# Keys and values of eight batches at a time in seven products, and every block's queries in seven products

## The chip, the core and the metric

The kernel runs on one core of one Trainium2 chip. The core has five engines that run side by side, each with its own queue of instructions worked off in order: TensorE (PE in the profile; its weight loads are listed as PEld), VectorE (DVE), ScalarE (ACT), GpSimd (POOL) and SyncE (SP), which here only issues DMA transfers. GpSimd issues a few transfers as well. The metric is the time of one execution on the device in microseconds (us), lower is better. An instruction waits, by semaphores, until what it reads is written and what it overwrites has been read.

## The reference

A cross-attention layer in float32 with 16 batches, 1024 query rows and 64 context rows per batch, width 512, 16 heads of 32:

```python
def _ada_ln(x, c, W_ss, b_ss):
    h = (x - mu) / jnp.sqrt(var + EPS)            # over the width
    ss = jax.nn.silu(c) @ W_ss + b_ss
    scale, bias = jnp.split(ss, 2, axis=-1)
    return (1.0 + scale)[:, None, :] * h + bias[:, None, :]

xq  = _ada_ln(x_q,  t_vec, Wss_q,  bss_q)         # 16 x 1024 x 512
xkv = _ada_ln(x_kv, t_vec, Wss_kv, bss_kv)        # 16 x   64 x 512
q = (xq @ Wq + bq).reshape(B, Lq, nh, dh)
kv = (xkv @ Wkv + bkv).reshape(B, Lkv, 2, nh, dh) # keys, then values
scores = jnp.einsum('bqhd,bkhd->bhqk', q, k) / jnp.sqrt(jnp.float32(dh))
attn = jax.nn.softmax(scores, axis=-1)
out = jnp.einsum('bhqk,bkhd->bqhd', attn, v).reshape(B, Lq, H)
return x_q + (out @ Wp + bp)
```

## The kernel before

**Tiling.** The 16x1024 query rows are cut into 32 blocks of 512 rows, two per batch, numbered 0 to 31. Keys and values are made for two batches at a time (128 context rows). All products are float32; a TensorE instruction of the program shows as two passes in the profile, so that four instructions of 256 columns are "x8".

**A block's path.** `load_x` brings the rows in. `q_stats` takes mean and variance on VectorE (L263, L264), `q_scale` makes the reciprocal deviation (two ScalarE steps, then four small ones), `hidden` normalises on ScalarE (L324). `turn` transposes 32x32 squares on VectorE (L503) and `move` brings the squares to their partitions in 16 transfers (L516), so that the features lie on partitions. `scale_features` puts in the batch's scale and shift (L573). Then the queries (`query_product` and what stands with it, L633 to L670), `scores` (two halves, each followed by a maximum on VectorE, L703, and a copy out of PSUM on ScalarE, L712), `maxima` (L725, L734), `subtract` on GpSimd (L747), `weights` (the exponential, L753), `total` (L792), `row_total` and `inverse_rows` (L797, L812, and a way through DRAM, L815 and L817), `mix` (the second attention product, `po`, L861), `spread_rows` and `divided` (L823, L841), and the projection (`product` and `added`, L976 and L1000), which adds into the residual that `load_residual` brought, and writes out.

**Seven products.** Queries (from block 4) and projections (all but block 29's) are made by a 2x2 scheme of seven half-size products in the place of eight, with sums of quarters of the weights (`query_weight_sums`, `weight_sums`, once) and of the features (`feature_sums`, four GpSimd additions per block, L608 to L611). Two PSUM banks hold running results; `query_out` reads them out on ScalarE, `query_added` adds on VectorE. Blocks 0 to 3 use the plain form (`queries`, L546): sixteen instructions of 512 columns. Blocks 0 and 1 use weights that already hold the batch's scale (`query_weights`), with the shift's part in the bias (`query_bias_rows`, L464).

**Keys and values before.** Per pair of batches: a load, a statistic as fifth entry beside a block's four, `context_hidden`, four transposes (L351, `pkt`), a scaling on VectorE (L369) and a shift on GpSimd (L373), 16 instructions for the keys (L398, `pk`), 64 small ones for the values (L434, `pv`), and additions of the biases (L409, L447). In the loop a pair is spread over four blocks, one step in each (`kv` 0 to 3).

**Order.** Everything is written out by hand and each engine works its queue in the order written; no scheduler moves anything. Blocks 0 to 3 have an order of their own; from block 4 on a loop runs:

```python
for i in range(4, NB - 2):
    a, b, n, f = i - 1, i - 2, i + 1, i + 2
```

In turn `i` TensorE does scores of block `i`, queries of block `n`, the second attention product and the start of the projection of block `a`, and the rest of the projection of block `b`, while the other engines prepare blocks `f`, `i + 3` and `i + 4`. A tail handles blocks 30 and 31. PSUM has two pairs of banks (pool `ps_s`) that scores and the second attention product take in turn, and four single banks (`mm0` to `mm3`).

## Time and profile before

| | |
|---|---|
| median of 3 runs | 1040.41 us (1039.51 to 1040.89) |
| span of the profiled execution, from its first to its last instruction | 1038.5 us |
| what lies around the span, by the median | 1.9 us |
| PE busy | 1019.3 us, 98% |
| DVE busy | 854.9 us, 82% |
| POOL busy | 780.9 us, 75% |
| ACT busy | 610.6 us, 59% |
| granted TensorE clock | 1.00 |
| HBM | 79.02 MB read, 34.60 MB written |

The page gives the profiled execution its span alone; its own time is read as the span and the 1.9 us that the median of the runs stands above it. A line of groups reads: source line, engine, operation, tiles written and read, shapes, count, then busy time, the mean of one, and the idle time of the engine just before with what ended it. The chain that ended last is followed back from the last instruction of the run; each of its pieces has a start, a length, and what ran or was waited for. "issue" is time for which the profile shows no reason.

### The profile page before, as it was taken

Reading aid. Unit: us, or ns where it says so; the run is one execution under the profiler, and the core shown is the slowest. Engines: PE = TensorE matmul, PEld = TensorE weight load, DVE = VectorE, ACT = ScalarE, POOL = GpSimd, SP = SyncE. Lnnn points to the kernel's source line nnn. Section 1 sums busy time; section 2 is a strip of 40 time slices with the busy share of each in tenths; the row PEclk is TensorE's granted clock in tenths of the full one; section 3 lists DMA queues with packets and bytes.
Section 4 is the critical chain, followed back from the end, with each engine's and each line's share of the span. In section 5 each row is a group of like instructions: output and inputs, shape, how many; then the busy total and the mean of one; then the engine's idle time right before and its main releaser. Section 6 shows DMA issues by size and latency. Waiting matters only on the chain.

```text
span 1038.5 us, 22968 instructions
## 1 busy us (share of the span) xinstructions
PE 1019.3 (98%) x9058; PEld 759.5 (73%) x9058; DVE 854.9 (82%) x1159; ACT 610.6 (59%) x945; POOL 780.9 (75%) x502
## 2 busy tenths in 40 slices
PE   6999899999999999999999999999999999999998
PEld 4535577778777778778778787777787778777756
DVE  5889978987798887897979877998778987776794
ACT  3666756665566745675657666566566665565530
POOL 0579786886978867988668986688886886977861
PEclk9999999999999999999999999999999999999999
DMA  9841555343455333545334445344444453235122
GB/s 338 262 150 62 164 168 182 117 154 117 144 173 164 118 101 135 165 160 164 102 105 163 155 150 160 100 136 146 140 158 138 127 158 112 100 123 165 45 85 85
DMA packets 103500, 147.65 MB, mean 142 GB/s; under 512 B 33464, under 2 KB 34640, under 8 KB 103392
## 3 DMA queue, kind: packets, MB, share of 16 engines
q1 hardware_dynamic: 102368, 144.08, 43.4%
q0 software_dynamic: 1024, 2.10, 0.9%
q8 instruction: 72, 1.18, 0.5%
q14 instruction: 36, 0.29, 0.1%
HBM read 79.02 MB, written 34.60 MB: 109 GB/s over the span
## 4 chain that ended last, share of the span: by engine, by line
PE 84%; DVE 7%; DMA 3%; POOL 3%; ACT 1%; issue 1%; SPq 0%; DVEq 0%; POOLq 0%
PE pp L976 34%; PE pq L633 33%; PE po L861 6%; PE ps L684 6%; PE pv L434 2%; PE pk L398 2%; DMA x<-in_x_dram 2%; DVE m L703 1%; DVE bs L263 1%; DVE l L758 1%; DVE vb L823 1%; DVE lt L797 1%; DMA vr<-ltd 1%; DVE ot L841 1%; DVE r L1000 0%
## 5 line engine op out<-in xcount | busy, mean ns | idle before, releaser
L747 POOL TENSOR_TENSOR s<-s,mb 128x2048 f32<-128x2048 f32 x62 | 281.3, 4561 | 167.3 <-DVE mb L734 163.3
L712 ACT COPY s<-ps 128x1024 f32<-128x1024 f32 x128 | 129.3, 1012 | 106.3 <-DVE m L703 67.0
L703 DVE TRANSPOSE_TENSOR_REDUCE m<-ps 128x32 f32<-128x1024 f32 x128 | 150.9, 1215 | 29.8 <-PE ps L684 27.6
L976 PE MATMUL pp<-w_p_sb,ot 128*128 128x256 f32 x744 | 171.0, 380 | 1.1 <-DVE ot L841 0.7
L1000 DVE TENSOR_TENSOR r<-pp,r 128x512 f32<-128x512 f32 x210 | 136.2, 670 | 30.3 <-PE pp L976 24.1
L663 ACT ACTIVATE qt<-pq,bias_t 128x256 f32<-128x256 f32 x224 | 92.4, 463 | 116.1 <-PE pq L633 116.1
L976 PEld LDWEIGHTS pp<-w_p_sb,ot 128*128 128x128 f32 x744 | 141.3, 190 | 21.7 <-issue 1.7
L753 ACT ACTIVATE s<-s 128x2048 f32<-128x2048 f32 x64 | 122.3, 1911 | 46.4 <-POOL s L747 44.4
L792 POOL TENSOR_TENSOR sum<-s,s 128x2048 f32<-128x2048 f32 x30 | 136.2, 4541 | 5.5 <-ACT s L753 5.5
L976 PEld LDWEIGHTS pp<-WT,s 128*128 128x128 f32 x496 | 89.7, 190 | 57.0 <-issue 34.4
L976 PE MATMUL pp<-WT,s 128*128 128x256 f32 x496 | 123.1, 391 | 0.4 <-POOL s L955 0.2
L976 PE MATMUL pp<-WT,ot 128*128 128x256 f32 x496 | 117.7, 381 | 1.2 <-POOL ot L952 1.2
L633 PE MATMUL pq<-xt_sums,wq_sums 128*128 128x256 f32 x448 | 108.5, 386 | 0.0
L633 PE MATMUL pq<-xt,w_q_sb 128*128 128x256 f32 x448 | 106.3, 380 | 2.1 <-ACT pq L645 1.8
L633 PEld LDWEIGHTS pq<-xt_sums,wq_sums 128*128 128x128 f32 x448 | 83.0, 190 | 32.4 <-issue 22.4
L633 PE MATMUL pq<-xt,wq_sums 128*128 128x256 f32 x448 | 106.6, 381 | 0.0
L976 PEld LDWEIGHTS pp<-WT,ot 128*128 128x128 f32 x496 | 94.0, 190 | 16.9 <-POOL ot L952 2.5
L324 ACT ACTIVATE x<-x,rstdq 128x512 f32<-128x512 f32 x128 | 96.5, 807 | 3.1 <-DVE rstdq L294 1.9
L670 DVE TENSOR_TENSOR qt<-pq,qt 128x256 f32<-128x256 f32 x112 | 42.1, 418 | 66.2 <-PE pq L633 65.7
L633 PEld LDWEIGHTS pq<-xt,w_q_sb 128*128 128x128 f32 x448 | 85.0, 190 | 15.1 <-ACT pq L645 2.2
L263 DVE BATCH_NORM_STATS2 bs<-x 128x6 f32<-128x512 f32 x128 | 86.9, 679 | 9.5 <-DMA x<-in_x_dram 9.5
L633 PEld LDWEIGHTS pq<-xt,wq_sums 128*128 128x128 f32 x448 | 83.6, 190 | 11.8 <-issue 1.2
(128 smaller groups left out, 1581.1 us busy)
## 6 DMA issues: line engine op xcount, KB each, us to landing
x<-in_x_dram SPq DMA_DIRECT2D x32, 1024.0 KB, 5.8
r<-in_x_dram SPq DMA_DIRECT2D x32, 1024.0 KB, 5.6
out_dram<-r SPq DMA_DIRECT2D x60, 512.0 KB, 3.7
xt<-ht SPq DMA_DIRECT2D x464, 64.0 KB, 2.0
wss_q<-in_L_xcond_Wss_q_dram SPq DMA_DIRECT2D x2, 1024.0 KB, 8.0
ctx<-in_ctx_dram SPq DMA_DIRECT2D x8, 256.0 KB, 3.3
wss_kv<-in_L_xcond_Wss_kv_dram SPq DMA_DIRECT2D x2, 1024.0 KB
w_kv_sb<-in_L_xcond_Wkv_dram SPq DMA_DIRECT2D x1, 2048.0 KB
```

The costliest lines, as they stand in the source:

```text
L263: nc.vector.bn_stats(bs, r)
L324: nc.scalar.activation(dst, src, AF.Identity, bias=rstd[:, 1, j : j + 1], scale=rstd[:, 0, j : j + 1])
L633: nc.tensor.matmul(qa[k][:, m * HT : (m + 1) * HT].rearrange("p (g n) -> p g n", g=2), lhsT=a[:, c, m * P : (m + 1) * P], rhs=x[:, :, c, : ...
L663: nc.scalar.activation(dst, src, AF.Identity, bias=bq_t[:, o : o + 1])
L684: nc.tensor.matmul(pss[r // 2][32 * c : 32 * c + 32, r % 2, :], lhsT=kt[rows, c, z * HK : (z + 1) * HK], rhs=qt[rows, c, :], start=True, s ...
L703: nc.vector.tensor_reduce(m_tiles[i][:, z, 2 * e : 2 * e + 2, :], pss[e].rearrange("p r (j a) -> p r j a", a=32), AX.X, ALU.max, apply_tra ...
L712: nc.scalar.copy(s_sb[:, 2 * e : 2 * e + 2, :], pss[e])
L747: eng.tensor_tensor(s_tiles[i, z], s_tiles[i, z], mb_tiles[i], ALU.subtract)
L753: nc.scalar.activation(p, p, AF.Exp, scale=SCALE)
L792: nc.gpsimd.tensor_tensor(t, s_tiles[i, 0], s_tiles[i, 1], ALU.add)
L976: nc.tensor.matmul(acc[k][:, t * HO : (t + 1) * HO], lhsT=rows[:, c, t * P : (t + 1) * P], rhs=cols[:, c, :], start=n == 2 and t == 0 and ...
L1000: nc.vector.tensor_add(r, a, r)
```

## The change

Context rows are treated like query blocks. Group A is batches 0 to 7, group B batches 8 to 15; each has 512 context rows and is loaded by `load_x`, has statistics and is normalised as a block. Keys and values of a group are made with seven products each (`seven`, `context_steps`), 28 sets of four instructions in all, and kept on chip (`K_all`, `V_all`) to the end. Group A's features are transposed by TensorE and scaled by VectorE as they leave PSUM (`turned_features`, `turned_scaled`, `group_affine`); group B's go the way of a block (`turn`, `move` with every second transfer on GpSimd's queue, then eight VectorE operations, `group_affine`). The values come out of the products in another order of partitions; they are put into a staging tile and brought to their places in 16 transfers per group (`value_move`). The steps of group A stand ahead of and among the queries of block 0, those of group B behind them and in the loop's places that have no projection yet. All queries are made in seven products; block 0's features are transposed by TensorE (`turned_queries`). The loop starts at block 0; the pair steps in it are gone. Block 0's projection takes the plain form into banks that hold the bias (`project_seed`, `project_seeded`); `weight_sums` moves to turn 1. The order of the loads changes, and several tiles share room: the key weights, value weights and their sums lie in buffers that scores and residuals use later, and the staging tiles in that of the projection's weight sums.

```diff
-    load_x(0)
-    load_scale_shift("q", w_ss_q)
-    nc.sync.dma_start(w_q_sb, w_q.rearrange("(c p) o -> p c o", p=P))
-    load_context(0)
-    load_x(1)
-    load_scale_shift("kv", w_ss_kv)
-    nc.sync.dma_start(w_kv_sb, w_kv.rearrange("(c p) o -> p c o", p=P))
+    load_x("A")
+    load_scale_shift("kv", w_ss_kv, 0)
+    load_biases()
+    load_scale_shift("kv", w_ss_kv, 1)
+    load_context_weights(0)
+    load_value_bias()
+    load_context_weights(1)
+    load_x(0)
+    load_scale_shift("q", w_ss_q, 0)
+    load_scale_shift("q", w_ss_q, 1)
...
+    def turned_scaled(i, t, pt):
+        xk = xt_tiles[i].rearrange("p g c (t b) -> p g c t b", t=NT)
+        src = pt.rearrange("p (c j n) -> p c j n", c=NC, j=2)
+        b = GROUPS[i] * PER + 2 * t
+        for j in range(2):
+            scale = ss["kv"][:, :NC, b + j : b + j + 1].unsqueeze(3).to_broadcast([P, NC, 2, 32])
+            nc.vector.tensor_tensor(
+                xk[:, 2 * j : 2 * j + 2, :, t, :].rearrange("p z c b -> p c z b"),
+                src[:, :, j, :].rearrange("p c (z b) -> p c z b", z=2),
+                scale,
+                ALU.mult,
+            )
+
+    def group_affine(i, g, shift, eng):
+        xk = xt_tiles[i][:, g].rearrange("p c (t b) -> p c t b", t=NT)
+        s = group_batches(i, NC if shift else 0, g // 2)
+        s = s.unsqueeze(3).to_broadcast([P, NC, NT, 32])
+        eng.tensor_tensor(xk, xk, s, ALU.add if shift else ALU.mult)
...
+    def value_move(i, m):
+        for c in (2 * m, 2 * m + 1):
+            for t in range(NT):
+                nc.sync.dma_start(
+                    V_all[i][32 * c : 32 * c + 32, 2 * t : 2 * t + 2],
+                    stages[i][32 * t : 32 * t + 32, c].rearrange("p (j z) f -> p j z f", j=2),
+                )
+
+    def context_steps(i, name, banks):
+
+        ks, vs = (key_out, key_added), (value_out, value_added)
+        out_, add_ = ks if name == "k" else vs
+        for n in (1, 2, 6, 7, 5, 4, 3):
+
+            def step(n=n):
+                seven(i, name, n, banks)
+                if i == "A" and n == 1:
+                    out_(i, n)
+                elif i == "A" and n == 2:
+                    add_(i, n)
+                elif n == 1:
+                    seed(i, name, banks)
+                elif n in OUTS:
+                    out_(i, n)
+                else:
+                    add_(i, n)
+
+            yield step
...
+    feature_sums("A", nc.vector)
+    both_of()
+    both_of()
     q_stats(0)
     q_scale(0)
     hidden(0, range(NT))
+    next(KA)()
     scale_shift_rows("q", 0)
     scale_shift_rows("q", 1)
+    scale_shift_taken("q")
+    next(VA)()
+    scale_shift("q", 0)
+    q_stats("B")
+    both_of()
+    turned_queries()
+    column_sums("q", w_q_sb, w_q_sums, nc.gpsimd)
+    load_x(1)
+    q_scale("B")
+    feature_sums(0)
+    both_of()
+    hidden("B", range(NT))
+    turn("B", range(NT))
+    move("B", two=True)
     load_x(2)
+    both_of()
     q_stats(1)
+    both_of()
+    query_product(0, 1)
+    query_seed(0)
     q_scale(1)
     hidden(1, (0, 1))
+    for g in range(2):
+        group_affine("B", g, False, nc.vector)
+        group_affine("B", g, True, nc.vector)
+    query_product(0, 2)
+    query_out(0, 2)
     hidden(1, (2, 3))
     turn(1, range(NT))
+    move(1, two=True)
...
+    next(KB)()
+    scale_features(1, (0, 1))
+    next(KB)()
+    scale_features(1, (2, 3))
+    feature_sums(1)
+    next(KB)()
     hidden(2, range(NT))
...
-    for i in range(4, NB - 2):
+    for i in range(NB - 2):
...
+        def slot(j, m):
+            if j > 0:
+                product(j, m)
+            elif j == 0:
+                if m in (1, 2, 6, 5):
+                    project_seeded(0, (1, 2, 6, 5).index(m))
+            else:
+                step = next(KB, None) or next(VB, None)
+                if step is not None:
+                    step()
         scores(i, 0, crossed=True)
+        if i == 0:
+            turn(2, range(NT))
+            move(2)
+            load_x(4)
-        product(b, 6)
-        added(b, 6)
+        slot(b, 6)
+        add(b, 6)
...
-        if kv == 1:
-            context_scaled(kvb)
-        if kv == 2:
-            key_products(kvb, spare(f"pk_{kvb}"))
-        if kv == 3:
-            value_products(kvb, spare(f"pv_{kvb}"))
...
         query_product(n, 5)
         query_added(n, 5)
+        if i == 0:
+            turn(3, range(NT))
+            load_x(5)
         if i + 4 < NB:
             q_stats(i + 4, (2,))
...
         query_product(n, 4)
         query_added(n, 4)
```

## The prediction

> **What bounds the kernel now.** I read the page's engine shares first, then the chain that ended last, then its pieces in order of time, then the busy time of four stretches. Page and chain:
>
> ```profile
> span 1038.5 us, 22968 instructions
> PE 1019.3 (98%) x9058; PEld 759.5 (73%) x9058; DVE 854.9 (82%) x1159; ACT 610.6 (59%) x945; POOL 780.9 (75%) x502
> PE 84%; DVE 7%; DMA 3%; POOL 3%; ACT 1%; issue 1%; SPq 0%; DVEq 0%; POOLq 0%
> ```
>
> TensorE's busy share is modelled, so the pieces of the chain (start, us, what) have to confirm it. `po` is a block's second attention product, one per block; the first here is block 3's, the last block 28's:
>
> ```profile
> 168.67 2.28 PE po L861 x62
> 197.85 2.28 PE po L861 x62
> 200.13 1.93 PE pq L633 x8
> 205.51 1.73 PE pq L633 x8
> 227.48 2.28 PE po L861 x62
> 236.86 3.57 PE pk L398 x32
> 260.24 2.28 PE po L861 x62
> 269.62 3.63 PE pv L434 x128
> 293.25 2.28 PE po L861 x62
> 945.49 2.28 PE po L861 x62
> ```
>
> From one `po` to the next: 29.18 us for a block that makes no keys or values, 32.76 and 33.01 for those with `pk` and `pv`. The differences, 3.58 and 3.83, are the TensorE pieces themselves: nothing else sets a block's length. So in the loop TensorE's instructions are the time. The stretches (columns: length, then PE, PEld, DVE, ACT, POOL busy, clock, DMA, GB/s) show where that is not so:
>
> ```profile
> 0.00:16.70 16.70, 7.07 (x91) 5.76 (x91) 7.12 (x25) 6.02 (x11) 0.70 (x6) 1.00 0.85 307
> 16.70:154.50 137.80, 134.82 (x1196) 81.35 (x1195) 118.99 (x175) 85.28 (x138) 99.43 (x85) 1.00 0.56 178
> 154.50:932.50 778.00, 777.84 (x6985) 602.85 (x6984) 654.43 (x880) 481.99 (x753) 613.37 (x380) 1.00 0.44 139
> ```
>
> Until 16.7 the loads are all that moves; 154.5 is the first score product of block 4, where the regular loop begins. VectorE is at 86% in the second stretch: it is the engine with the least room while the pipeline fills.
>
> **The change, part by part.** Sums are against the profiled span, 1038.5; the median of the timed runs, 1040.41, is 1.9 above it, and I carry that 1.9 over.
>
> TensorE work. (1) Removed from the loop: six pairs of batches. Block 3's `po` to block 28's is 776.82 us; 25 blocks at 29.18 are 729.5, so the six cost 47.3 (7.9 each). Two more pairs, in the opening, at 0.43 (`pkt`) + 3.57 + 3.63: 15.3. (2) Added: 4 sets (two groups, keys and values) of seven products; a set is 6x1.73 + 1.93 = 12.3 (the loop's query set): 49.2; group A's 16 transposes at 0.43 per four: 1.7. (3) Queries of blocks 0 to 3: the plain form took 14.00 per block (piece at 47.85, 32 passes), seven products 12.3: -6.8. (4) The query-bias product of L464 goes (-1.1); block 0's projection becomes the plain form, 14.0 for 12.3 (+1.7). Net: -62.6 + 50.9 - 6.8 + 0.6 = -17.9. All of it is on the path, if TensorE is kept fed.
>
> The additions of keys and values are priced by L670 (418 ns) and L409 (658 ns). The other engines in the loop lose work (L369, L409, L447, L373 and a statistic): worth nothing, since the 29.18 blocks are TensorE's without them.
>
> The opening. Before, TensorE runs from 16.7 to 154.5 with 132.0 of work (4x14.0 + 12.3 queries, 15.3 keys and values, 8.6 scores, 6.8 `po`, 29.8 projections, 3.2 small): 5.8 us of waits. After, the work up to block 4's first scores is 132.0 - 6.8 + (49.2 - 15.3) + 0.6 + 1.7 (block 0's transposes, which ran before 16.7 and now run behind the first keys; group A's run before its first product) = 161.4. I lay the queues out with before's row times:
>
> - Start. Loads drain in order at about 3.0 us per MB: block 2's x had 10.25 MB issued up to its end and landed at 33.7.
>
> ```profile
> 16.82 16.92 DMA x<-in_x_dram
> ```
>
> The context's second scale-and-shift weight is the third MB: 12.2. Then 1 us of rows, 12 transposes, the bias add, eight 0.41 us scalings (price of L670's 418 ns) and two shifts put the first key product at 20.5. Cost: +3.8.
> - Block 0's scale rows wait for a VectorE copy. VectorE: POOL's two shifts done 22.6, four sums to 25.9, three additions to 28.2, block 0's statistics (4x0.77) to 31.3, its scale (two ScalarE and four VectorE steps, 1.5) 32.8, the copy 33.2; TensorE is there at 32.7: 0.5.
> - Block 1's x is issued when block 0's transposes free its buffer (38.8) and lands at 44.5; its statistics stand behind group A's additions (48.7 to 51.8), its scale ends at 53.2, and hidden(1), four steps of 0.81, stands on ScalarE between the query_out of block 0 (0.46 each). Block 0's products, 1.73 apart from 49.2, wait 0.6 for the seed, 0.8 for the first copy out, 0.8 for the second: 2.2.
> - Group B: its features move half by POOL's queue (8 DMAs, 3.91 us in before's row, 4.9 to landing), then eight VectorE affines, then POOL's feature sums (4x1.27) behind the eight DMAs of block 1's move. In numbers: turn(B) done 47.3, POOL's moves landed 56, affines to 57.7 and 64.1, turn(1) 60.5, its POOL DMAs to 64.5, third sum 68.3; the product is due at 67.4: 0.9.
> - scores(0, 1) needs the PSUM pairs of scores(0, 0), whose copies stand on ScalarE behind hidden(2): block 1's odd moves land at 69.4, its scaling and group B's outs run to 74.6, hidden(2) to 77.8, two copies (1.01) to 79.8; the scores are due at 76.3: 3.5.
> - Block 0's turn of the loop. VectorE carries two blocks' statistics (6.2), two turns (5.4), maxima (7.5), both groups' additions and a row total (2.8): about 28 us in a 31 us turn, in order. POOL's subtractions run from 86.4 (2x4.56), the second exponential ends at 97.4, the query_out behind it at 98.3: product 4 (due 96.5) is 1.8 late. Half a scaling and hidden(3) end at 103.1, turn(3) at 103.9, a statistic and query_added(1, 4) at 105.5: scores(1, 0), due 103.5, 2.1 late. A statistic, an addition, row_total(0) and its reciprocal (4.3) stand ahead of the maxima (2.5), which end at 112.4: scores(1, 1), due 110.1, 2.3 late. Together 6.2.
> - Block 1's turn: maxima, spread of the maxima and of the inverse sums (2.3 each) and two `ot` halves (1.22) end at 124.2; the seeded projection is due at 122.7: 1.5. Block 1's `ot` is 0.8 late in the same way.
> - Transfers. SP's sixteen issues of a move take 10.35 us in the loop; the two value moves add 32 issues of the same size (64 KB), 20.7 us of SP. Ahead of block 4's x and block 0's residual they make these land at about 95 and 130, 0 to 2 us after need, on VectorE and not on TensorE: 0.
>
> ```profile
> 314.63 10.35 SPq L516 DMA_DIRECT2D xt<-ht  x16
> ```
>
> Waits: 0.5 + 2.2 + 0.9 + 3.5 + 6.2 + 2.3 = 15.6. Block 4's scores then start at 20.5 + 161.4 + 15.6 = 197.5, 43.0 later than before. The rest loses 47.3, and block 4's own 1.2 over a regular block (30.4 between its scores and the next) may go too; I count half. Sum: +43.0 - 47.3 - 0.6 = -4.9: span 1033.6, time 1035.5.
>
> Unshown costs. VectorE's all-SBUF 128x512 operations (two shifts, four sums, eight affines): from 0.67 (L1000, one operand in PSUM) to 0.84 (a quarter of L747's 3342 ns); taken near the middle; ends -1 and +1 us on the path. The waits together: from before's 5.8, if the order hides as well as before's, to twice mine, 31: the end moves by -9.8 and +15.6. I take 15.6, since each of its terms follows from a row and an in-order queue, and keep the ends for the range. The start: from 18.5 (no queueing of the small loads) to 23: -2 and +2.5.
>
> What VectorE's all-SBUF work does to POOL is seen at one place: while VectorE ran its only two subtractions, POOL's fourth weight sum took 3.32 for a usual 1.27.
>
> ```profile
> 53.92 6.61 DVE L747 TENSOR_TENSOR s<-s,mb 128x2048 f32<-128x2048 f32 x2
> 55.06 3.32 POOL L918 TENSOR_TENSOR WT<-w_p_sb,WT 128x512 f32<-128x512 f32 x1
> 58.35 2.78 POOL L919 TENSOR_TENSOR b_diff<-b_p_sb 128x256 f32<-128x256 f32 x1
> ```
>
> With L919 (2.78; half of 1.27 by size) POOL lost some 4.2 us in 6.6. The change adds about 10 us of such VectorE work, so POOL may lose 6; group A's part hides (the value sums are due 4 us later), group B's 3 falls on its feature sums or block 1's DMAs: 0 to 3 us, taken as 0, since the affines mostly end before POOL's work starts. [...]
>
> **The rivals.**
>
> A. The order hides the fill (waits 5.8 as before): 1035.5 - 9.8 = 1026. For it: queues laid out by hand serialise more than the chip does. Against it: three of the waits come from in-order queues, whatever the durations.
>
> B. Slower, by POOL's queue. Group B's and block 1's odd moves go through it in a row: landing 4.9 is a median of 32, and SP's own moves reach 8.1. If POOL's take 8.1 too, group B's last affine and turn(1) slip 3.2, block 1's features another 3.2, hidden(2) and the copies of scores(0, 0) by 6.4, and TensorE with them; with the 3 us that VectorE may take from POOL, by 9.4: 1045. It decides from a slip of 7.0, which puts the time 2.1 past before's 1040.4; below that it only eats the gain. For it: nothing else in the opening can run meanwhile, as TensorE's order has only group B's products there. Against it: group B's features have 5 us of slack at their first product, and the landing is a median.
>
> C. The loop's blocks do not fall to 29.18, another engine being just behind. The 29.18 blocks are in this trace, with VectorE at 84%: 0.05 at most; at 29.5 the 25 blocks would add 8: 1043.
>
> **How the numbers follow.** A change of 0.2% (2.1 us) is about what a measurement of this kernel tells from none. Forecast (1029 to 1038): 0.46; A: 0.20; B: 0.25, a fifth of it within the bound; C: 0.05; a near miss of the forecast between 1038.3 and 1042.5: 0.04. Faster 0.66, same 0.09, slower 0.25. Range: below, A with the early start and the rest of block 4's 1.2, 1023; above, B with contention and 2 us, 1047.
>
> **What would show it.** Key and value groups of 28 products in all, none after block 1; `po` 29.2 apart from block 4 on, everywhere; first key product near 20.5; block 4's scores near 198. Before that, TensorE idle ahead of scores(0, 1) released by ScalarE's copies, ahead of scores(1, 0) by VectorE. Wrong if scores(4, 0) stands past 202 (slower) or before 190 (A), or if a regular block is not 29.2.

## The result, and the profile after

The changed kernel is 0.5% slower: median 1047.03 us of 12 runs, against 1040.97 of the kernel before, beside it on the same chip; the ratio is 1.0051, interval 1.0038 to 1.0064. The forecast was 1035.5.

The page of the changed kernel (span, engine shares, PE and granted clock in forty slices, the chain by engine):

```profile
span 1044.6 us, 21070 instructions
PE 1007.0 (96%) x8025; PEld 759.3 (73%) x8025; DVE 877.8 (84%) x1184; ACT 628.1 (60%) x980; POOL 806.4 (77%) x504
PE   3988899999999999999999999999999999999997
PEclk8999999999999999999999999999999999999999
PE 83%; DVE 5%; DMA 3%; SPq 3%; ACT 2%; POOL 2%; issue 1%; DVEq 0%; POOLq 0%
```

TensorE has 12.3 us less work than before (1019.3) in a span 6.1 us longer. The dents of PE's row, and the clock's only one, lie in the first five slices (26 us each). The pieces of the chain in order of time:

```profile
4.04 7.04 DMA early<-in_L_xcond_bss_kv_dram
18.34 5.38 issue
23.72 3.71 PE pk_A L504 x8
27.43 1.73 PE pv_A L504 x8
...
220.72 2.42 PE po L798 x63
...
951.19 2.28 PE po L798 x62
```

220.72 is block 3's second attention product, 951.19 block 28's: 730.5 us, where the kernel before took 776.82. The loop gained 46.3; the forecast said 47.3. What was lost was lost earlier: block 4's scores start at 207.8 (forecast 197.5, kernel before 154.5), and from there to the end are 836.8 us (before: 884.0). The first key product starts at 23.72 (forecast 20.5) and takes 3.71 us; the next, of the same size, takes 1.73. Four stretches (columns as before: length, then PE, PEld, DVE, ACT and POOL busy, clock, DMA, GB/s):

```profile
18.50:23.70 5.20, 0.00 (x0) 0.01 (x1) 5.09 (x11) 0.00 (x0) 4.75 (x5) 0.69 1.04 387
23.70:27.50 3.80, 3.78 (x10) 3.03 (x11) 2.90 (x2) 0.03 (x1) 3.72 (x4) 0.53 1.04 387
...
180.00:960.00 780.00, 780.00 (x6415) 596.17 (x6414) 686.42 (x893) 508.81 (x789) 649.58 (x398) 1.00 0.47 143
```

TensorE stands idle for 5.2 us, then gets 0.53 of its clock for 3.8; from 180 on it is busy in every microsecond. The timeline of the same execution, four engines in the opening:

```profile
24.57 1.74 DVE L468 TENSOR_TENSOR xk_sums_A<-xk_A 128x512 f32<-128x512 f32 x1 [0.95 <-POOL xk_A L424]
26.34 1.64 DVE L469 TENSOR_TENSOR xk_A<-xk_A 128x512 f32<-128x512 f32 x1
...
37.73 1.18 DVE L299 SCALAR_TENSOR_TENSOR workq<-mvq,workq 128x4 f32<-128x4 f32 x1
...
93.58 9.01 POOL L689 TENSOR_TENSOR s<-s,mb 128x2048 f32<-128x2048 f32 x2 [8.27 <-DVE mb L676]
...
98.15 4.45 DVE L299 SCALAR_TENSOR_TENSOR workq<-mvq,workq 128x4 f32<-128x4 f32 x1
...
101.64 1.52 ACT L429 ACTIVATE xt<-xt,ss_q 128x512 f32<-128x512 f32 x2 [0.87 <-DMA xt<-ht]
103.06 1.89 ACT L695 ACTIVATE s<-s 128x2048 f32<-128x2048 f32 x1
105.82 3.62 PE L504 MATMUL pq<-xt_sums,w_q_sb 128*128 128x256 f32 x8 [3.00 <-ACT qt L543]
```

Two readings. VectorE's additions of two SBUF operands (L468, L469, two more alike) take 1.64 to 1.74 us, not the 0.67 to 0.84 of the forecast, and a step on 128x4 numbers, elsewhere 0.16, takes 1.18 and 4.45: beside them GpSimd works. And product 4 of block 1's queries waits 3.0 us for ScalarE's copy out of product 7, which stands behind the second exponential (L695). Two chains meet there: GpSimd's subtraction ends at 102.6, and on ScalarE the scaling of block 2's features (L429), which has waited 0.87 us for block 2's moves on SP, ends at 103.2, so that the moves are the later by 0.6. Then product 4 runs at half speed (3.62 for 1.9; the granted clock is 0.50 from 106 to 109).

### The profile page after: what moved, and what is told of

It is laid out like the page before. It is cut to its first block, busy times and chain, and to the rows that moved or that the text cites. A ratio compares the mean times of both kernels' runs of the same rounds, so it can differ in the third digit from the quotient of the medians.

```text
span 1044.6 us, 21070 instructions
## 1 busy us (share of the span) xinstructions
PE 1007.0 (96%) x8025; PEld 759.3 (73%) x8025; DVE 877.8 (84%) x1184; ACT 628.1 (60%) x980; POOL 806.4 (77%) x504
## 4 chain that ended last, share of the span: by engine, by line
PE 83%; DVE 5%; DMA 3%; SPq 3%; ACT 2%; POOL 2%; issue 1%; DVEq 0%; POOLq 0%
PE pq L504 34%; PE pp L928 34%; PE ps L628 6%; PE po L798 6%; SPq L364 2%; POOL s L689 1%; DMA b_p_sb<-in_L_xcond_bp_dram 1%; DVE bs L277 1%; ACT s L695 1%; PE pk_A L504 1%; DMA early<-in_L_xcond_bss_kv_dram 1%; DVE m L645 1%; DMA r<-in_x_dram 1%; ACT x L318 1%; DMA x<-in_x_dram 1%
## 5 line engine op out<-in xcount | busy, mean ns | idle before, releaser
L689 POOL TENSOR_TENSOR s<-s,mb 128x2048 f32<-128x2048 f32 x64 | 290.3, 4560 | 144.8 <-DVE mb L676 130.7
L928 PE MATMUL pp<-w_p_sb,ot 128*128 128x256 f32 x720 | 165.4, 379 | 2.4 <-DVE ot L778 1.9
L543 ACT ACTIVATE qt<-pq,bias_t 128x256 f32<-128x256 f32 x256 | 105.6, 463 | 81.7 <-PE pq L504 81.7
L695 ACT ACTIVATE s<-s 128x2048 f32<-128x2048 f32 x64 | 122.3, 1911 | 46.2 <-POOL s L689 46.2
L504 PE MATMUL pq<-xt_sums,w_q_sums 128*128 128x256 f32 x512 | 123.9, 385 | 1.0 <-ACT qt L543 1.0
L504 PEld LDWEIGHTS pq<-xt_sums,w_q_sums 128*128 128x128 f32 x512 | 94.8, 190 | 37.7 <-issue 24.8
L504 PE MATMUL pq<-xt,w_q_sb 128*128 128x256 f32 x512 | 121.1, 379 | 0.7 <-ACT pq L516 0.7
L504 PE MATMUL pq<-xt,w_q_sums 128*128 128x256 f32 x512 | 121.1, 379 | 0.1
L504 PEld LDWEIGHTS pq<-xt,w_q_sb 128*128 128x128 f32 x512 | 97.2, 190 | 15.1 <-ACT pq L516 1.1
L504 PEld LDWEIGHTS pq<-xt,w_q_sums 128*128 128x128 f32 x512 | 97.2, 190 | 14.0 <-ACT qt L543 0.8
L429 ACT ACTIVATE xt<-xt,ss_q 128x512 f32<-128x512 f32 x124 | 94.0, 809 | 2.5 <-DMA xt<-ht 1.4
```

The source lines that it names most:

```text
L429: nc.scalar.activation(xt[:, :, c, :], xt[:, :, c, :], AF.Identity, scale=ss["q"][:, c, b : b + 1], bias=ss["q"][:, NC + c, b : b + 1],)
L504: nc.tensor.matmul(out_, lhsT=lhsT, rhs=rhs, start=new and m == 0 and c == 0, stop=c == HC - 1, skip_group_check=True,)
L543: nc.scalar.activation(dst, src, AF.Identity, bias=bq_t[:, o : o + 1])
L689: eng.tensor_tensor(s_tiles[i, z], s_tiles[i, z], mb_tiles[i], ALU.subtract)
L695: nc.scalar.activation(p, p, AF.Exp, scale=SCALE)
L928: nc.tensor.matmul(acc[k][:, t * HO : (t + 1) * HO], lhsT=rows[:, c, t * P : (t + 1) * P], rhs=cols[:, c, :], start=n == 2 and t == 0 and ...
```

## The experiments

All experiments edit the changed kernel, and all ratios are against the kernel before, run beside them (1040.7 to 1041.4). With an unchanged start, scores(0, 0) begins anywhere from 77.9 to 80.1, so differences of a microsecond between single traces say nothing. The starts of the first halves of the scores (us), each from the one profiled execution of its run, and the ratios of the medians; the names are explained below:

| kernel | block 0 | block 1 | block 2 | block 4 | ratio (interval) |
|---|---|---|---|---|---|
| changed | 78.6 | 112.8 | 146.4 | 207.8 | 1.0051 (1.0038 to 1.0064) |
| x4 early | 80.1 | 117.3 | 150.1 | 211.5 | 1.0077 (1.0060 to 1.0094) |
| scale on GpSimd | 78.7 | 112.8 | 145.7 | 207.1 | 1.0062 (1.0046 to 1.0079) |
| both | 78.1 | 114.2 | 146.7 | 208.1 | 1.0071 (1.0056 to 1.0086) |
| warm | 79.6 | 114.1 | 147.2 | 208.6 | 1.0061 (1.0046 to 1.0076) |
| subtraction | 77.9 | 115.7 | 149.1 | 210.6 | 1.0097 (1.0082 to 1.0112) |
| no value moves | 78.1 | 110.8 | 147.8 | 209.2 | 1.0046 (1.0029 to 1.0063) |
| hidden(2) later | 78.1 | 112.4 | 145.2 | 207.2 | 1.0062 (1.0047 to 1.0077) |
| statistics first | 76.2 | 110.2 | 143.8 | 206.1 | 1.0052 (1.0031 to 1.0072) |
| order 1 | 76.9 | 104.6 | 152.7 | 214.1 | 1.0118 (1.0103 to 1.0133) |
| order 1, warm | 75.7 | 103.4 | 150.9 | 212.2 | 1.0103 (1.0087 to 1.0120) |
| order 2 | 75.4 | 103.0 | 142.7 | 205.8 | 1.0053 (1.0038 to 1.0068) |
| order 3 | 75.5 | 103.2 | 140.3 | 208.0 | 1.0028 (1.0017 to 1.0040) |
| order 4 | 75.0 | 102.6 | 140.3 | 203.8 | 0.9996 (0.9984 to 1.0007) |
| order 5 | 74.8 | 102.5 | 136.8 | 201.2 | 0.9968 (0.9954 to 0.9983) |

### Is it SP's queue in block 0's turn? (x4 early, scale on GpSimd, both)

**x4 early.** Block 4's x is loaded ahead of block 2's moves:

```diff
+            load_x(4)
             move(2)
-            load_x(4)
```

> Block 4's x load is put ahead of the 16 moves of block 2 on SP's queue, nothing else changes. Theory SP (the transfers' order on SP's queue is what the opening lost most to): block 4's x lands near 94 us in place of 105.7, VectorE's statistics wait for nothing, the 3.2 us that TensorE waits ahead of query product 4 of block 1 and the half clock behind it (1.7 us) go: span 4.9 us shorter, about 1040. Rival, GpSimd's subtraction holds VectorE's small operations of block 3's scale (4.45 us for one of 0.17): VectorE is held to 102.8 anyway and only the 1.8 us from there to the landing are won: span 1 to 2 us shorter.

Slower. The x landed in time, and VectorE came free no earlier, since its long step (L299, 4.45 us) stood there still; block 2's moves came later behind the load, with them the scaling on ScalarE (104.69 for 101.64), the second exponential behind it and the copy out of product 7. Product 4 waited 4.55 us. The theory that the late landing of block 4's x is the price fell; but SP's queue counts here through another transfer, block 2's moves.

**Scale on GpSimd.** Block 3's small scale steps leave VectorE:

```diff
-        apart = i not in GROUPS and i > 3
+        apart = i not in GROUPS and i > 2
```

> Block 3's four small scale steps run on GpSimd, as those of the later blocks do, in place of VectorE. Theory SP: nothing is won, VectorE is free at 98 us but waits for block 4's x to 105.7: span 1044.6 within 1 us. Rival GpSimd-holds-VectorE as the sole cause: the 4.3 us are won at once, span about 1040.

The 4.45 us step is gone, product 4 still waits 2.87 us, and nothing is gained: the ratio is that of the changed kernel within its interval.

**Both.** The two edits together:

> Both edits together. If the two causes stand one behind the other, the gain is more than the sum of the two alone: x of block 4 at 94, VectorE free at 98, product 4 of block 1 waits only for the query_out behind the second exponential (due 102.4, about 103): 4.9 us or a little more, span 1038 to 1040, and if the next waits (block 0's residual, the maxima) shorten with it, 1036. If only SP's order counted, the same as that edit alone.

VectorE now stood idle for 5.0 us, waiting for ScalarE. Product 4 still waited 3.47 us. ScalarE's timeline:

```profile
101.61 1.52 ACT L429 ACTIVATE xt<-xt,ss_q 128x512 f32<-128x512 f32 x2 [1.34 <-DMA xt<-ht]
103.04 1.89 ACT L695 ACTIVATE s<-s 128x2048 f32<-128x2048 f32 x1
```

GpSimd's subtraction had ended at 102.1. So in block 0's turn the last links are second exponential, copy out of product 7, product 4, and VectorE does not end last. What the second exponential waits for is the scaling of block 2's features, and so block 2's moves; the subtraction (9.0 us) ends 0.6 us before the scaling in the changed kernel and 1.0 here. The same holds for every single edit but the one without value moves.

### Is the half clock a price of its own? (warm)

```diff
     scale_shift("kv", 2 * NC)
+    warm = bank("warm", 1)
+    for _ in range(6):
+        nc.tensor.matmul(warm, lhsT=ident, rhs=w_k_sb[:, 0, :], start=True, stop=True)
```

> Six extra products of the identity with key weights, into a bank that nothing reads, fill TensorE's idle 18.3 to 23.7 us. Theory clock (the half clock after a wait costs what it adds): the first key product takes 1.73 us in place of 3.71 and the span falls by 2.0. Rival: behind it TensorE waits for VectorE's chain to the copy at 39.2 us anyway, the product's gain is waited away there: the clock is 1.00 in 23.7 to 27.5 but the span stays within 0.5 us.

The clock was 1.00 and the first key product took 1.97. But the time did not fall (1047.43 for 1047.03), as TensorE then waited for VectorE's copy of the scale rows, and paid the clock there (3.54 us for 1.89; 0.90 of the clock from 27.5 to 45). The timeline of this run:

```profile
39.05 0.44 PE L265 MATMUL ss_q<-ident,early 128*128 128x128 f32 x2 [3.69 <-DVE early L258]
39.32 3.54 PE L504 MATMUL pk_A<-xk_sums_A,w_k_sums 128*128 128x256 f32 x8
```

### The subtraction, the value moves, hidden(2)

**Subtraction.** Block 0's subtraction on VectorE (in the place of GpSimd), block 3's scale steps behind GpSimd's sum, x4 early, half of block 2's moves on GpSimd's queue:

```diff
-            move(2)
             load_x(4)
+            move(2, two=True)
...
-        subtract(i)
+        subtract(i, nc.vector if i == 0 else nc.gpsimd)
...
-        if i == 0:
-            q_scale(3)
         weights(i, 0)
...
         total(i)
+        if i == 0:
+            q_scale(3)
```

> Block 0's subtraction on VectorE in place of GpSimd (block 3's scale steps behind it), block 4's x load ahead of block 2's moves, and these moves half on GpSimd's queue, which is then free. Theory softmax chain (in block 0's turn the way subtraction, second exponential, query_out 7, query product 4 sets the end, whatever the transfers do): the subtraction takes 6.6 us for 9.0, the exponential's data are there 2.5 to 3 us earlier, the 3.2 us wait and the 1.7 us of half clock go for the most part: block 4's scores 3 to 5 us earlier, span 1040 to 1042. Rival, VectorE as a whole is what block 0's turn lacks: the 6.6 us that it takes over come back behind it (additions, turn of block 3): span 1044 to 1048.

VectorE did the subtraction in 4.5 us for both halves, half of GpSimd's time, and it ended at 97.3. The gain was lost twice: the second exponential started at 100.8 (103.1 in the changed kernel), as ScalarE waited 1.57 us for block 2's moves ahead of it, and the scale steps of block 3 then met GpSimd's sum, and the addition of product 5 (L550) stood behind them. VectorE's timeline:

```profile
103.65 3.67 DVE L298 SCALAR_TENSOR_TENSOR workq<-workq 128x4 f32<-128x4 f32 x1
107.35 1.18 DVE L299 SCALAR_TENSOR_TENSOR workq<-mvq,workq 128x4 f32<-128x4 f32 x1
108.57 0.16 DVE L300 SCALAR_TENSOR_TENSOR rstdq<-workq 128x4 f32<-128x4 f32 x1
108.76 1.11 DVE L301 SCALAR_TENSOR_TENSOR rstdq<-rstdq,mvq 128x4 f32<-128x4 f32 x1
```

A step that needs 0.16 us alone held VectorE for 3.67, to 107.3, about where GpSimd's sum ends: it follows the second exponential, which ends at 102.7, and takes 4.54 us in the changed kernel.

**No value moves.** The 32 transfers of `value_move` are left out; the values stay zero:

```diff
+    for g in GROUPS:
+        nc.gpsimd.memset(V_all[g], 0.0)
...
-    value_move("A", 1)
-    value_move("A", 0)
...
-            value_move("B", 1)
-            value_move("B", 0)
```

> The 32 transfers that bring the values to their places are left out (the values are zeros set at the start on GpSimd; the output is wrong by that), everything else is as in the changed kernel. Theory SP: block 4's x lands some 10 us earlier and block 0's residual too, span 3 to 5 us shorter. Theory softmax chain: SP's 20 us were not on the path, span shorter by 1 us at most.

Block 0's turn got shorter by 1.5 us: block 2's moves were no longer late behind the value moves on SP, and the second exponential waited 0.45 us for the subtraction alone. Block 1's got longer by 3.5, in it a wait of 3.05 us. The ratio is that of the changed kernel within the intervals, so the forecast's price for these transfers, 0, is not refuted for the time; for block 0's turn it was not 0.

**hidden(2) later**, behind the copies of scores(0, 0) on ScalarE:

```diff
-    hidden(2, range(NT))
...
         if i == 0:
+            hidden(2, range(NT))
             turn(2, range(NT))
```

> hidden(2) stands behind the copies of block 0's first scores on ScalarE and not ahead of them. If the order on ScalarE costs what the prediction said of it, scores(0, 1) start 1.4 us earlier (the wait seen there) and the maxima, the subtraction and the second exponential follow: span 1 to 2 us shorter. Rival: block 2's features come 2 us later by it, their scaling stands ahead of the second exponential, and the gain is lost there: within 0.5 us.

Counted from scores(0, 0), scores(0, 1) came 1.3 us earlier, scores(1, 0) not at all. The subtraction ended at 100.4 (102.6 in the changed kernel), but the scaling now waited 2.35 us for block 2's moves, and product 4 waited 4.49.

### Is VectorE's queue the start's price? (statistics first)

```diff
+    q_stats(0)
     feature_sums("A", nc.vector)
     both_of()
     both_of()
-    q_stats(0)
```

> Block 0's statistics stand on VectorE ahead of group A's four feature sums, where VectorE waits 1 us for GpSimd, and not behind group A's additions. Theory VectorE chain (the start is late by VectorE's all-SBUF work beside GpSimd's weight sums, up to the copy of the scale rows at 39.2): the copy comes 1.5 to 2.5 us earlier and scores(0, 0) and the end with it, span 1042 to 1043. Rival, something later in the opening sets the end anyway (the softmax chain does not depend on when block 0 starts only if its start moves too, so it should not): span unchanged within 0.5 us; or the third sum is late for the third key product and takes 1 us back.

Blocks 0 to 2 came 2.4 to 2.6 us earlier, block 4 by 1.6, as block 2's turn gave 0.9 back; product 4 still waited 3.13 for the chain of block 0's turn. The median stands 0.5 below the changed kernel's, which is inside the intervals: the earlier start is shown, a shorter time is not. The run shows what slows the additions, since GpSimd ends its sums (L448 to L451) in the middle of them. Its timeline, VectorE and then GpSimd:

```profile
26.89 1.65 DVE L469 TENSOR_TENSOR xk_A<-xk_A 128x512 f32<-128x512 f32 x1
28.57 1.64 DVE L470 TENSOR_TENSOR xk_sums_A<-xk_A 128x512 f32<-128x512 f32 x1
30.24 0.69 DVE L471 TENSOR_TENSOR xk_sums_A<-xk_A,xk_sums_A 128x512 f32<-128x512 f32 x1
...
26.26 1.72 POOL L450 TENSOR_TENSOR wv_sums<-w_v_sb 128x512 f32<-128x512 f32 x1
27.95 1.71 POOL L451 TENSOR_TENSOR wv_sums<-w_v_sb,wv_sums 128x512 f32<-128x512 f32 x1
```

Beside GpSimd 1.65 and 1.64, after it 0.69; GpSimd's own take 1.7 beside VectorE and 1.27 alone. In the run "order 1", where GpSimd is idle by then, all four take 0.66 to 0.69.

### Order or load? (order 1 to 5)

What stayed open was whether the opening's loss lies in the order of the queues or in an engine's load. So the work was kept (but for the six products of "warm") and its order changed, one late queue after another; a few operations also went to another engine or queue.

**Order 1** puts the statistics first, hidden(2) later and, in block 0's turn, cuts the chain: the copy out of product 7 and the second exponential stand ahead of block 2's scaling (and the work that was due there, `row_total(0)`, `turn(3)` and `move(3)`, moves into block 1's turn). Two places of it:

```diff
+        if i == 1:
+            turn(3, range(NT))
+            move(3)
+            load_x(5)
...
+        if i < 2:
+            query_product(n, 7)
+            query_out(n, 7)
         weights(i, 1)
         total(i)
-        query_product(n, 7)
-        query_out(n, 7)
+        if i == 0:
+            scale_features(f, (0, 1))
+        if i > 1:
+            query_product(n, 7)
+            query_out(n, 7)
```

> The products are those of the changed kernel; only the order is another, in two places. Start: block 0's statistics stand ahead of group A's feature sums, the little bias transposes behind the second set of scale rows, all four additions of A's shift are on VectorE. Block 0's turn: hidden(2) stands behind the copies of scores(0, 0); block 3's scale steps are GpSimd's; the copy out of product 7 stands ahead of the second exponential, the copy out of product 3 ahead of hidden(3); block 4's statistics stand behind product 4's addition; row_total(0), turn(3) and move(3) come in block 1's turn (the same order of product 7's copy there). Theory (two chains, each with its own price: VectorE at the start, subtraction and second exponential in block 0's turn): first key product 23.0 or earlier, scores(0, 0) near 75 (78.7 in the changed kernel), scores(1, 0) between 104 and 107 (112.9), block 4's scores between 199 and 203 (207.8), so a time of 1038 to 1042. Rival (the fill is bound by something that all single edits left, so that every gain is waited away): block 4's scores stay at 205 or later, 1044 or more.

Order 1 with the six products of "warm":

> The kernel of the run beside it, with six products of the identity and w_k (their result unused) behind the scale and shift transposes, so that TensorE does not stand idle ahead of the first key product. Theory (half clock after an idle time of over 3 us is a price of its own, 1.7 to 2.0 us, which the warm run above lost only because VectorE's copy was late anyway): clock 1.00 through the first key product, block 4's scores 1.5 to 2.5 us earlier than in the run beside it. Rival (the clock's price is waited away further down in any order): the same within 0.7 us.

Block 0's turn fell from 34.2 us to 27.7; what of it is the chain and what the work that left the turn, the run does not separate. Block 1's turn rose from 33.5 to 48.1. In it, move(3) now stood ahead of block 0's residual load on SP. The timeline of order 1, SP and VectorE:

```profile
121.98 11.08 SPq L364 DMA_DIRECT2D xt<-ht  x16
133.17 0.52 SPq L119 DMA_DIRECT2D x<-in_x_dram  x1
133.80 1.02 SPq L126 DMA_DIRECT2D r<-in_x_dram  x2
...
142.22 0.69 DVE L855 TENSOR_TENSOR r<-pp,r 128x512 f32<-128x512 f32 x1 [15.12 <-DMA r<-in_x_dram]
```

VectorE stood for 15.1 us. The warm products beside it gained 1.2 us at block 0's scores, 1.8 at block 4's and 1.9 in the median (1052.89 to 1050.99; no time of the one kernel reaches the other's, four of each), in an order in which VectorE's copy is not late; so the half clock is a price of its own (mean granted clock 0.994, for 0.990 in order 1).

**Order 2** (warm, as are all that follow) loads the residual first and takes product 7 of block 2 ahead of block 0's projection:

```diff
+        if i == 1:
+            load_residual(0)
+            move(3)
+            load_x(5)
...
+        if i == 1:
+            query_product(n, 7)
+            query_out(n, 7)
         if i > 0:
             scale_features(f, (0, 1))
```

> The kernel of the run before this (new order and warm clock) with block 1's turn put right: block 0's residual load stands on SP's queue ahead of the sixteen moves of block 3 (in the run before it landed 15 us late and VectorE stood for it), turn(3) follows row_total(0) on VectorE, and product 7 of block 2 with its copy out stands ahead of block 0's projections. Theory (each turn of the fill is set by its own last chain, and a residual load behind a move was block 1's): scores(1, 0) as before this edit near 103.3, scores(2, 0) near 136 (150.8 in the run before, 146.4 in the changed kernel), block 4's scores between 196 and 200, a time of 1035 to 1040, thus at or below the kernel before. Rival (another wait in block 1's turn takes the place): scores(2, 0) at 141 or later, time 1042 or more.

Block 1's turn: 39.7 us. Two waits of TensorE were left that in-order queues make: 2.68 us for an addition of values behind turn(3), 2.50 for the addition of product 5, behind the statistics of a block whose x landed at 133.5.

**Order 3** moves these, and gives two of group A's additions back to GpSimd:

```diff
+        slot(b, 6)
+        add(b, 6)
         if i == 1:
             row_total(0)
             inverse_rows(0)
             turn(3, range(NT))
-        slot(b, 6)
-        add(b, 6)
+            load_x(5)
...
+        if i == 1:
+            query_product(n, 6)
         if a >= 0:
             mix(a)
```

> The kernel of the run before this with four more moves: block 5's x is loaded right behind turn(3), ahead of block 3's moves (it landed at 133.5 and held VectorE, and with it the addition of product 5); group B's fifth value product and its addition stand ahead of row_total(0) and turn(3) (TensorE waited 2.8 us for that addition); product 6 of block 2 stands ahead of block 0's attention product; two of group A's four additions are GpSimd's again. Theory (each wait of the fill has its own last chain, and VectorE's is the last at the start): scores(0, 0) near 73.5 (75.3 in the run before), scores(2, 0) between 134 and 138 (142.6), block 4's scores between 196 and 200 (205.7), a time of 1036 to 1041, so at or a little below the kernel before. Rival (VectorE's load between scores(1, 0) and scores(2, 0) is the bound, in any order): scores(2, 0) at 140 or later, time 1043 or more.

Block 2's scores came in at 140.3, on the rival's side. Block 3's scaling, which waited 4.9 us for its moves on ScalarE, held the second exponential of block 1, and the chain from there cost block 2's turn a wait of 3.24 us; from block 2's scores to block 4's it took 67.7 us, where order 2 took 63.1. The median fell to 1044.74.

**Order 4** puts that exponential ahead of the scaling, and loads x4 early as in the first experiment, now that in block 0's turn no scaling stands ahead of the exponential; half of group B's values go through GpSimd's queue:

```diff
-            move(2)
             load_x(4)
+            move(2)
...
-        if i > 0:
+        if i == 1:
+            weights(i, 1)
+            total(i)
+        if i > 1:
             scale_features(f, (0, 1))
```

> The kernel of the run before this with its two remaining stalls addressed. Block 0's turn: block 4's x is loaded ahead of block 2's moves, so that its statistics run where VectorE stood idle (2.8 us), block 2's scaling stands behind the copy out of product 3, hidden(3) behind the copies of scores(1, 0). Block 1's turn: the second exponential and the sum of the weights stand ahead of block 3's scaling (which waited 4.9 us for its moves on ScalarE), half of group B's values goes through GpSimd's queue. Theory (the fill is bound by the order of the queues, not by an engine's load): scores(2, 0) between 135 and 138.5 (140.4 in the run before), scores(2, 1) 5 later, no wait over 3 us ahead of block 3's scores, block 4's scores between 196 and 201 (208.2), a time of 1035 to 1041. Rival (VectorE's load between scores(1, 0) and scores(2, 0) is the bound): scores(2, 0) at 139.5 or later, and a time that stays at or above the kernel before's.

The time of the kernel before, 1040.54. The early load that cost 2.6 us alone (1049.66 for 1047.03) stands in an order that is 4.2 us faster than the last, and VectorE uses it: block 4's statistics run from 94.6 to 97.9, where it stood idle for 2.9 us. What the load alone gives in this order was not measured. scores(2, 0) did not move, and its wait is in the timeline (VectorE, TensorE):

```profile
133.72 2.49 DVE L342 STREAM_TRANSPOSE ht<-x 128x512 f32<-128x512 f32 x4 [2.88 <-DMA xt<-ht]
136.14 0.71 DVE L550 TENSOR_TENSOR qt<-pq,qt 128x256 f32<-128x256 f32 x2
...
136.91 2.84 PE L504 MATMUL pq<-xt,w_q_sums 128*128 128x256 f32 x8 [4.15 <-DVE qt L550]
```

turn(4) waited for block 3's moves to leave its tile, the addition stood behind turn(4), and TensorE behind the addition.

**Order 5** puts turn(4) behind the additions of products 5 and 4:

```diff
-        if 0 < i < NB - 3:
+        if 1 < i < NB - 3:
             turn(i + 3, range(NT))
...
         query_added(n, 4)
+        if i == 1:
+            turn(4, range(NT))
+            load_x(6)
```

> The kernel of the run before this with turn(4) of block 1's turn behind the additions of products 5 and 4, not ahead of them (there it waited for block 3's moves to leave its tile, and TensorE waited 4.3 us for the addition behind it, then ran at part of its clock for about 3 us). Theory (order of the queues): no wait over 2 us in block 1's turn, scores(2, 0) near 134.5 (140.4 in the run before), block 4's scores between 196.5 and 199.5 (203.8), a time of 1033 to 1037, which is faster than the kernel before by 0.3 to 0.7%. Rival (another late queue takes its place): scores(2, 0) at 138 or later, time within 2 us of the run before.

1038.30 us (11 runs), ratio 0.9968, interval 0.9954 to 0.9983: 0.3% faster than the kernel before, and 8.7 us faster than the changed kernel, with its work and six products more. Its page, and two stretches of block 1's turn:

```profile
span 1037.8 us, 21106 instructions
PE 1009.7 (97%) x8037; PEld 759.2 (73%) x8037; DVE 870.7 (84%) x1180; ACT 628.8 (61%) x983; POOL 810.5 (78%) x516
```

```profile
134.20:136.80 2.60, 0.11 (x1) 0.00 (x0) 2.57 (x7) 2.60 (x6) 1.46 (x2) 0.92 1.08 353
136.80:144.60 7.80, 7.77 (x40) 2.88 (x41) 4.97 (x4) 3.34 (x8) 7.49 (x7) 0.59 0.80 238
```

The engines are as busy as in the changed kernel (VectorE 870.7 against 877.8, GpSimd 810.5 against 806.4). So no engine's load bound the changed kernel: with nearly the same load, another order is 8.7 us faster. Even this order does not reach the forecast's 197.5 for block 4's scores; turn 1 still pays a wait of 2.6 us and 7.8 us at a clock of 0.59.

## Why the prediction was wrong

**Right: the ledger of TensorE's work in the loop, and what bounds it.** Six pairs at 7.9 us were to go; 46.3 us went, of 47.3, and from block 4's scores to the end it took 836.8 where the forecast's sum has 836.1 (1033.6 less 197.5). A block is 29.2 us, as in the blocks before that had no key or value step. TensorE's work in all was to fall by 17.9: PE's busy time fell by 12.3, and with 3.7 of half clock (below) taken off, by 16.0; the slow first products (below), of which the changed kernel has more (two sets at 1.94 us, where one of before's two took 1.08), make about 1 more. Rival C is out. Rival B (GpSimd's DMA queue) is out too: the transfers of group B's move took 2.0 to 3.1 us to land, not the forecast's 4.9 or the rival's 8.1, and its key products waited 0.66 us for a copy of ScalarE and 0.23 for GpSimd's sums. That the rival's 1045 lies near the measured time is therefore luck.

**Wrong: the opening, 43.0 us later than before by forecast, 53.3 in fact.** The 10.3 between, by steps of the forecast. A wait is counted here, as in the forecast, by what it adds from one product's start to the next beyond the 1.73 us of four instructions back to back, which is some 0.16 us more than the idle time in the timeline:

1. "put the first key product at 20.5": 23.7, +3.2; in six runs whose edits lie behind it, it came at 22.3 to 23.2, so that up to 1.4 of this belongs to the one execution. The small loads of biases, behind a load of 1 MB, landed only at 11.1 (7.04 us in the chain above), and scale rows and transposes queued behind the small transposes that need them. "1 us of rows": the 32 row products took 1.94 us both times. The additions of the shift took 1.07 each beside GpSimd. What such rows cost at the start stood in the trace of the kernel before (its first two sets, then the changed kernel's):

```profile
10.19 1.94 PE L234 MATMUL pss_q<-wss_q,early 128*32 128x128 f32 x32 [2.32 <-DVE mvq L264]
14.47 1.08 PE L234 MATMUL pss_q<-wss_q,early 128*32 128x128 f32 x32
...
11.42 1.94 PE L245 MATMUL pss_kv<-wss_kv,early 128*32 128x128 f32 x32
14.33 1.94 PE L245 MATMUL pss_kv<-wss_kv,early 128*32 128x128 f32 x32
```

   The granted clock reads 1.00 over all four sets, but three of them take 1.94 us and one 1.08.
2. No term for the clock: the first key product at 0.53 of it, +2.0. The table of the kernel before gives 1.00, and so do its stretches up to 205 us, so only the two sets of rows above, 1.94 and 1.08 us, could have shown what a slower TensorE costs; the change made long idle times behind the start. A second such stretch, 1.7 behind product 4's wait, is counted in point 4.
3. "the copy 33.2; TensorE is there at 32.7: 0.5": the copy ended at 39.7. Of the 6.5, some 2.0 are the start's, 3.4 are the four sums (6.7 us for 3.3) and 1.2 the scale, two steps of which were slowed. TensorE lost 1.7, so +1.2. Up to the first query product the loss is 6.3, which these three make up (6.4).
4. "Waits: 0.5 + 2.2 + 0.9 + 3.5 + 6.2 + 2.3 = 15.6", without the first: block 0's queries 2.25 (forecast 2.2), group B 1.2 (0.9), scores(0, 1) 1.4 (3.5), from there up to scores(1, 1) 7.0 (6.2; in it 1.7 for the clock), the rest up to block 4's scores 5.5 (2.3). In sum 17.4 for 15.1, +2.3. Some 1.6 are spread over gaps too small to place.

So the step that failed is the sum of the opening, "20.5 + 161.4 + 15.6 = 197.5": 207.8 was measured. Its start was 3.2 short, it had no term for the clock (3.7 in two stretches), and its waits were 1.2 short at the copy and 0.6 short behind it without the clock, with the split wrong (block 1's turn and what follows 5.5 for 2.3, scores(0, 1) 1.4 for 3.5). One mechanism it had wrong is the one on "VectorE's all-SBUF 128x512 operations ... taken near the middle", with the sentence that GpSimd's loss beside them is "0 to 3 us, taken as 0"; it makes point 3 and a part of point 1, and how much of the end it makes no run shows. The row that showed it was quoted (L918 at 3.32 for 1.27), but it was read as GpSimd's loss alone, at group B. It goes both ways: VectorE's 0.69 becomes 1.65 and GpSimd's 1.27 becomes 1.72 (statistics first), and a step of VectorE of 0.16 up to 4.45 (changed kernel). Another is the step that let SP's value moves delay only block 4's x and block 0's residual: they stand ahead of block 2's moves as well, and through ScalarE's order these reach TensorE.

The second failure is of method. Waits were added up as if each were a price; the runs show that a single one taken away mostly comes back one station later: -1.3 us at scores(0, 1) became 0 at scores(1, 0), -2.4 at block 0 became -1.6 at block 4. None of the eight single edits made the time clearly shorter; the five orders, which took late queues away in a row, did, after a first one that was 5.9 us slower.

Rival A (the order hides the fill, 1026) is not what the changed kernel does; order 5 goes part of the way, at 1038.3. What stays open is how the loss in the changed kernel divides among the late queues, since only the clock's price was taken away alone and seen in the time.

## What to carry to other kernels

When a change takes work out of a loop and puts it into the opening, the loop's gain can be read off to a microsecond, and the opening has to be laid out in queues with the prices of engines that work side by side: here an operation of VectorE with two SBUF operands took about 2.4 times its time alone beside GpSimd's sums (1.64 us for 0.69), and a step on 128x4 numbers 4.45 for 0.16 beside an instruction of GpSimd of 4.5. In the changed kernel the products behind idle times of TensorE of 5.40 and 3.00 us took 2.0 and 1.7 us longer, at a granted clock of 0.53 and 0.50. Single edits in a fill with several in-order queues tell which chain ends last, not what the order is worth: follow the last chain, move it, look again; an edit that loses alone (x4 early) can stand in a faster order.

## What the runs showed of the hardware that was not expected

- TensorE ran at part of its clock behind waits of 5.40 and 3.00 us (changed kernel: 0.53 from 23.7 to 27.5, 0.50 from 106 to 109), 3.69 (warm: 0.90 from 27.5 to 45, a product in it at 3.54 us for 1.89), 2.52 (order 5: 0.59 over 7.8 us) and 1.52 (order 3: 0.74 over 6.6 us), but not behind 2.59 (no value moves: the product behind it took 1.96 us) and 3.13 (statistics first: 1.97 us, 1.00 from 80 to 110). So the length of the wait alone does not decide; what else does is not shown.
- The start is slow too: before, in the changed kernel, in statistics first and in order 2 the first 32 row products take 1.93 to 1.94 us; the second set takes 1.08 before and in order 2, and 1.94 in the changed kernel and in statistics first. The mean granted clock of a profile, 1.00 there, does not show it.
- GpSimd and VectorE hold each other up in both directions: in statistics first VectorE's addition takes 1.65 us for 0.69 and GpSimd's 1.72 for 1.27 side by side.
- The six products without use cost nothing that the time shows (1047.43 for 1047.03) and gained 1.9 us in the median in order 1, where TensorE would otherwise have stood idle ahead of real work.
